# The end of a four-layer image kernel: result transposes cut into pieces, scaled products ahead of the shift, and three result parts stored as one transfer each

## The chip, the cores and the metric

The kernel runs on one core of one Trainium2 chip. The metric is the device time of one execution in microseconds (us), of which the median over several executions is taken. For the kernel before there are three: 2442.64, 2442.99 and 2450.58 us, so the median is 2442.99 us.

## The reference

Four layers work on an image batch `x` of shape (4, 64, 64, 64), float32: a self-attention over the 4096 tokens of each image, a gated convolution block, a second attention, and a non-local block. Only the end of the last layer is touched here:

```python
y = jnp.einsum('bnm,bmd->bnd', f, g_x).reshape(B, H, W, INNER)   # f: softmax of theta . phi
w_y = jnp.einsum('bhwd,dc->bhwc', y, w_W) + w_b
mean = jnp.mean(w_y, axis=(0, 1, 2))
var = jnp.var(w_y, axis=(0, 1, 2))
w_y = gamma * (w_y - mean) * jax.lax.rsqrt(var + EPS) + beta
return x + w_y
```

The mean and the variance run over all four images. So nothing can be stored before the last projection (`w_y`) of the last image is there; after that, all 4.19 MB of the result have to be scaled, shifted, added to `x`, turned and written to HBM.

## The kernel before

**Tiles.** `X` holds the input of the last layer for all four images, channels on partitions: 128 partitions (two halves `p` of the image by 64 channels) by 2048 columns for each image. `wys[b]` holds `w_y` in the same way. The result is cut into eight parts, two for each image: part `i` is 1024 columns of image `i // 2`. The result lies in HBM with the channel last, so each part must be turned by TensorE in eight blocks of 128x128 before it is stored.

**PSUM.** One tile `PS` of 128x4096 is dealt out in slots of 1024 columns. `take_slots` says which slots the next `new_ps` calls go round; the fourth slot serves `new_acc` for small sums.

**The end, in order.** `close_last` (line 1773) finishes the last 512 columns of the last image in two halves of 256: the softmax divisor by Ln and Exp on ScalarE (L1779, L1780), three VectorE operations (L1784 to L1787), the projection on TensorE (`project`, L1756), the bias on ScalarE (L1790), and the statistics on VectorE (L1796). `finish` (line 1898) joins the statistics (L1901), sends them through TensorE to get both halves' values (L1903, L1904), and makes `scale` and `shift`, one number for each channel (L1910 to L1920).

**The first three parts** go a different way from the other five. Their blocks of `X` are turned early: `begin_out` (line 1882) multiplies each block by the identity into a PSUM slot and leaves the sum open (`stop=False`). It is called for part 0 in `close_last` before the projections (L1781), for part 1 at the start of `finish` (L1899), for part 2 after the small products (L1908). When `scale` is there, `end_out` (line 1929) adds each block of `w_y` times `dscale`, the diagonal matrix of `scale`, to the same sum (L1931); `dshift`, the diagonal matrix of `shift`, times `ones` gives the shift along a row (`acc2`, L1989), and `add_shift` (line 1953) adds it on VectorE (L1957) into an SBUF tile `o` and stores that.

**The other five parts** are scaled and shifted on ScalarE (L1986), added to `X` on VectorE (`add`, L1974), turned on TensorE (`turn_out`, L1981), copied to SBUF (L2004, and L2007 and L2009 for the last), and stored.

**Stores.** `store` (line 1936) builds the destination `dst` with the dimensions p (2), h (64), q (8), n (128). In HBM a step of p is 2048 elements, a step of h is 4096, and q and n together are 1024 neighbouring elements, 4 KB. In the tiles of the first three parts the 128 partitions are p outside and h inside; in the tiles of the other five, `by_p` puts h outside and p inside. For the first three, two transfers of 64 partitions each are issued from SP's queue (L1940):

```python
for p in range(2):
    nc.sync.dma_start(
        out=dst[p].rearrange("h q n -> h (q n)"), in_=o[64 * p : 64 * p + 64, 0:1024]
    )
```

For the others it is one transfer of 128 partitions with h outside and p inside (L1944), from SP's queue for parts 3 and 5 and ScalarE's for 4 and 6, and two halves for part 7 (L1948), one from each queue.

**Order.** Every engine runs its instructions in the order in which the code issues them (a manual schedule for TensorE, ScalarE, VectorE and GpSimd). After `finish` each engine loads the flag `bad` (L2023) and branches around a fallback path (L2024), then the core's engines meet at the end (L2059).

Of the kernel before, what the change touches and what calls it, by code (L numbers as in the profile page):

```python
# [691 lines left out]
def fast_path(ctx: ExitStack, tc: tile.TileContext, a: dict, out: bass.AP, bad):  # L692
    nc = tc.nc
# [50 lines left out]
    def new_acc():  # L744
        turn_of["acc"] += 1
        return PS[:, bass.ts(6 + turn_of["acc"] % 2, 512)]
# [92 lines left out]
    for nm in names64 + names32:  # L839
        n = flat[nm].shape[0]  # L840
# [788 lines left out]
    def layer3(b):  # L1629
# [123 lines left out]
        def project(yz, ps, c0, cols):  # L1753
            for k in range(4):
                s, jj = k // 2, k % 2
                mm(  # L1756
                    ps[64 * s : 64 * s + 64, 512 * jj : 512 * jj + c0], wo[32 * k : 32 * k + 32, :],
                    yz[32 * k : 32 * k + 32, cols], start=True, stop=True,
                )
# [13 lines left out]
        def close_last():  # L1773
            yz, inv, wy = new_t("yz"), new_t("inv"), wys[b][:, 1024:2048].rearrange("p (j n) -> p j n", j=2)
            inside(0, sums0.rearrange("p b t -> p (b t)"), LO, HI)
            inside(1, sums2.rearrange("p b t -> p (b t)"), LO, HI)
            for i in range(2):
                r = inv[:, bass.ts(i, 256)]
                act(r, st["z"][:, bass.ts(i, 256)], AF.Ln)  # L1779
                act(r, r, AF.Exp, scale=-1.0)  # L1780
            early.append(begin_out(0))  # L1781
            for i in range(2):
                cols, r, d = bass.ts(i, 256), inv[:, bass.ts(i, 256)], inv[:, 512 + 256 * i : 768 + 256 * i]
                nc.vector.tensor_mul(d, st["z"][:, cols], r)  # L1784
                k = 2 * b + 1 + i
                stt(d, d, -2.0, r, ALU.add, ALU.mult, accum_out=inv3[:, k : k + 1])
                stt(yz[:, cols], d, -1.0, st["y"][:, cols], ALU.mult, ALU.mult)  # L1787
                ps = new_ps()
                project(yz, ps, 256, cols)
                act(  # L1790
                    wy[:, :, cols], ps.rearrange("p (j n) -> p j n", j=2)[:, :, 0:256],
                    AF.Identity, bias=V("L3_conv_w_b"),
                )
            inside(2, inv3, -1.0 / LO, 0.0)
            for i in range(2):
                nc.vector.bn_stats(bst[:, b, 1, i, :], wy[:, :, bass.ts(i, 256)])  # L1796
# [82 lines left out]

    def begin_out(i):
        b, g = i // 2, i % 2
        if i == 0:
            take_slots(0, 1, 2)
        ps = new_ps()
        if i == 0:
            take_slots(1, 2)
        elif i == 2:
            take_slots(0, 1, 2)  # L1890
        for k in range(8):
            mm(
                ps[:, bass.ts(k, 128)], X[:, b, 1024 * g + 128 * k : 1024 * g + 128 * k + 128], ident,
                start=k % 4 == 0, stop=False,
            )
        return ps

    def finish():
        early.append(begin_out(1))  # L1899
        mv = sm.tile([128, 2], F32, tag="mv", name="mv")  # L1900
        nc.vector.bn_aggr(mv, bst.rearrange("p b n i s -> p (b n i s)"))  # L1901
        acc = new_acc()
        mm(acc[:, 0:2], half[:, 0:128], mv, start=True, stop=True)  # L1903
        mm(acc[:, 2:3], half[:, 128:256], mv[:, 0:1], start=True, stop=True)  # L1904
        inside(3, mv[:, 1:2], 0.0, HI)
        found = new_acc()
        mm(found[0:1, 0:4], ones[:, 0:1], good, start=True, stop=True)
        early.append(begin_out(2))  # L1908
        mean = sm.tile([128, 4], F32, tag="mean", name="mean")
        nc.vector.tensor_copy(mean[:, 0:3], acc[:, 0:3])  # L1910
        stt(mean[:, 3:4], mean[:, 2:3], mean[:, 2:3], mean[:, 1:2], ALU.mult, ALU.add)
        rstd = sm.tile([128, 1], F32, tag="rstd", name="rstd")
        act(rstd, mean[:, 3:4], AF.Ln, bias=eps3)
        act(rstd, rstd, AF.Exp, scale=-0.5)
        mg = sm.tile([128, 1], F32, tag="mg", name="mg")
        stt(mg, mean[:, 0:1], -1.0, V("L3_conv_gamma"), ALU.mult, ALU.mult)
        scale = sm.tile([128, 1], F32, tag="scale", name="scale")
        nc.vector.tensor_mul(scale, rstd, V("L3_conv_gamma"))
        shift = sm.tile([128, 1], F32, tag="shift", name="shift")
        stt(shift, rstd, mg, V("L3_conv_beta"), ALU.mult, ALU.add)  # L1920
        t = new_t("diag")
        dscale, dshift, shifts = t[:, 0:128], t[:, 128:256], t[:, 256:384]
        nc.vector.tensor_scalar_mul(dshift, ident, shift)
        nc.vector.tensor_scalar_mul(dscale, ident, scale)

        def part(i):
            return X[:, i // 2, bass.ts(i % 2, 1024)], wys[i // 2][:, bass.ts(i % 2, 1024)]

        def end_out(i):
            for k in range(8):  # L1930
                mm(  # L1931
                    early[i][:, bass.ts(k, 128)], part(i)[1][:, bass.ts(k, 128)], dscale,
                    start=False, stop=k % 4 == 3,
                )

        def store(i, o, half_=None):
            dst = out[i // 2].rearrange(by_rows, p=2, q=16)[:, :, bass.ts(i % 2, 8)]
            if i < E:
                for p in range(2):
                    nc.sync.dma_start(  # L1940
                        out=dst[p].rearrange("h q n -> h (q n)"), in_=o[64 * p : 64 * p + 64, 0:1024]
                    )
            elif half_ is None:
                (nc.sync if i % 2 else nc.scalar).dma_start(  # L1944
                    out=dst.rearrange("p h q n -> h p (q n)"), in_=o[:, 0:1024]
                )
            else:
                (nc.scalar if half_ else nc.sync).dma_start(  # L1948
                    out=dst[:, :, bass.ts(half_, 4)].rearrange("p h q n -> h p (q n)"),
                    in_=o[:, bass.ts(half_, 512)],  # L1950
                )

        def add_shift(i):
            o = new_e("o")
            if i == 0:
                nc.vector.tensor_copy(shifts, acc2[:, 0:128])
            nc.vector.tensor_add(  # L1957
                o[:, 0:1024].rearrange("p (k n) -> p k n", n=128),
                early[i].rearrange("p (k n) -> p k n", n=128),
                shifts.unsqueeze(1).to_broadcast([128, 8, 128]),  # L1960
            )
            store(i, o)

        def by_p(x):
            return x.rearrange("c (q p h) -> c q p h", p=2, h=H)

        E, os, pss = len(early), {}, {}

        def add(i):
            if i == 2 * B - 2:  # L1970
                os["last"] = new_big("o")
            os[i] = new_e("o") if i < 2 * B - 2 else os["last"][:, bass.ts(i % 2, 2048)]
            xs, ws = part(i)
            nc.vector.tensor_add(  # L1974
                os[i][:, 1024:2048].rearrange("c (q h p) -> c q p h", p=2, h=H), by_p(xs), by_p(ws)
            )

        def turn_out(i):
            pss[i] = new_ps()
            for k in range(8):  # L1980
                nc.tensor.transpose(  # L1981
                    pss[i][:, bass.ts(k, 128)], os[i][:, 1024 + 128 * k : 1152 + 128 * k], ident
                )

        for i in range(E, 2 * B):
            act(part(i)[1], part(i)[1], AF.Identity, bias=shift, scale=scale)  # L1986
        acc2 = new_acc()
        for o in range(2):
            mm(acc2[64 * o : 64 * o + 64, 0:128], ones, dshift, start=True, stop=True)  # L1989
        end_out(0)  # L1990
        end_out(1)
        end_out(2)
        for i in range(E):
            add(E + i)
            add_shift(i)
            if i == 0:
                nc.vector.tensor_reduce(cnt, found[0:1, 0:4], AX.X, ALU.add)
                nc.vector.tensor_scalar(bad, cnt, -1.0, float(counted[0]), ALU.mult, ALU.add)
        for i in range(E, 2 * B):
            turn_out(i)  # L2000
            if i + E < 2 * B:
                add(i + E)
            if i < 2 * B - 1:
                nc.scalar.copy(os[i][:, 0:1024], pss[i])  # L2004
                store(i, os[i])
        i = 2 * B - 1
        nc.vector.tensor_copy(os[i][:, 0:512], pss[i][:, 0:512])  # L2007
        store(i, os[i], 0)
        nc.scalar.copy(os[i][:, 512:1024], pss[i][:, 512:1024])  # L2009
        store(i, os[i], 1)  # L2010
# [52 lines left out]
```

## Time and profile before

| What | us |
|---|---|
| median of three runs | 2442.99 |
| the profiled execution's own time | 2444.88 |
| its span in the trace | 2443.1 |
| last exponentials done (ACT L1657), end | 2408.5 |
| first TensorE block of part 0 (L1892), start | 2412.64 |
| last statistics joined (DVE L1901), start | 2417.39 |
| `shift` ready and ScalarE's scaling begins (ACT L1986) | 2420.01 |
| last compute (ACT L2009), end | 2433.50 |

Times in the table from the third row on are counted from the span's start. TensorE is busy for 2410.9 us of the span (99%), but the stretch that the change touches is the last 30 us, in which the engines wait for each other and, after 2433.5 us, only transfers, branches and the final meeting are left. How to read it: find which instruction each stage waits for last, and then ask of the transfers when they start, how many of the 16 DMA engines carry them, and at what rate.

### The profile page before, as it was taken

How to read it: one execution, taken by the hardware profiler on the slowest of the kernel's cores; microseconds unless marked ns; L12 is line 12 of the kernel's file. 1: busy time of each engine (PE TensorE's matmuls, PEld its weight loads, DVE VectorE, ACT ScalarE, POOL GpSimd, SP SyncE). 2: the span in 40 equal slices, each digit the busy share in tenths (PEclk: the TensorE clock that was granted, in tenths of full speed). 3: DMA queues.
4: the chain of work that ended last, by engine and by line, in shares of the span. 5: the costliest groups of instructions: out<-in, count | busy, mean ns of one | idle time of the engine just before them, and what ended most of it. 6: DMA issues, size and time to landing. Idle time of an engine off the chain costs nothing.

```text
span 2443.1 us, 63650 instructions
## 1 busy us (share of the span) xinstructions
PE 2410.9 (99%) x27509; PEld 914.5 (37%) x27509; DVE 1477.5 (60%) x1794; ACT 1642.9 (67%) x3140; POOL 541.1 (22%) x381
## 2 busy tenths in 40 slices
PE   9999999999999999999999999999999999999998
PEld 3343453336333543343344442144421344421113
DVE  2020278227732774278657668876668866688886
ACT  4656766666666666668655459954479744569996
POOL 2000000000000000030136561256631365622110
PEclk9999999999999999999999999999999999999999
DMA  3000000000000000030540027610075300386554
GB/s 80 1 18 1 19 1 18 18 19 1 19 18 5 15 19 18 21 76 2 118 92 19 20 64 138 139 28 23 16 152 118 79 22 21 76 169 141 118 116 117
DMA packets 66373, 131.68 MB, mean 54 GB/s; under 512 B 12860, under 2 KB 34085, under 8 KB 66085
## 3 DMA queue, kind: packets, MB, share of 16 engines
q0 software_dynamic: 23024, 81.83, 16.6%
q1 hardware_dynamic: 42309, 43.85, 7.9%
q8 instruction: 218, 3.57, 0.6%
q10 hardware_dynamic: 752, 1.85, 0.2%
q14 instruction: 70, 0.57, 0.1%
HBM read 4.80 MB, written 4.19 MB: 4 GB/s over the span
## 4 chain that ended last, share of the span: by engine, by line
PE 87%; DVE 5%; ACT 4%; DMA 1%; issue 1%; SPq 1%; POOL 0%; ACTq 0%; DVEq 0%; POOLq 0%
PE PS L1096 18%; PE PS L1122 18%; PE PS L1391 10%; PE PS L1453 10%; PE PS L1646 8%; PE PS L1707 8%; PE PS L1479 7%; PE PS L1206 2%; DVE tg L1698 2%; ACT e L1657 2%; DMA xn<-e 1%; ACT e L1396 1%; PE PS L1064 1%; PE PS L1171 1%; PE PS L1270 1%
## 5 line engine op out<-in xcount | busy, mean ns | idle before, releaser
L1101 ACT ACTIVATE e<-PS 128x1024 f32<-128x1024 f32 x512 | 523.7, 1023 | 339.8 <-PE PS L1096 306.5
L1396 ACT ACTIVATE e<-PS 128x512 f32<-128x512 f32 x632 | 370.9, 595 | 330.2 <-PE PS L1391 312.5
L1096 PE MATMUL PS<-X,q 64*64 64x512 f32 x4096 | 574.0, 591 | 2.3 <-DVE X L979 1.7
L1122 PE MATMUL PS<-e,vq 64*64 64x512 f32 x4096 | 575.3, 592 | 0.0
L1657 ACT ACTIVATE e<-PS 128x512 f32<-128x512 f32 (+2 forms) x588 | 500.1, 920 | 60.3 <-PE PS L1646 38.0
L1698 DVE TENSOR_TENSOR tg<-tg,e 128x2048 f32<-128x2048 f32 x172 | 393.9, 2290 | 42.7 <-ACT e L1657 31.3
L1391 PE MATMUL PS<-ko 64*64 64x512 f32 x2528 | 335.6, 596 | 1.7 <-ACT ko L1313 0.8
L1453 PE MATMUL PS<-e,X 64*64 64x512 f32 x2528 | 329.6, 590 | 1.1 <-ACT own L1465 1.1
L1432 POOL TENSOR_TENSOR esum<-esum,e 128x1024 f32<-128x1024 f32 x132 | 314.1, 2380 | 60.0 <-ACT e L1396 52.7
L1241 DVE SCALAR_TENSOR_TENSOR y<-pad,vec,y 128x1024 f32<-128x1024 f32 x240 | 308.9, 1287 | 18.2 <-ACT y L1237 10.9
L1432 POOL TENSOR_TENSOR esum<-e 128x1024 f32<-128x1024 f32 x22 | 52.2, 2373 | 1192.5 <-ACT e L1396 1184.7
L1409 DVE STREAM_TRANSPOSE turned<-e 128x1024 f32<-128x1024 f32 x196 | 240.6, 1238 | 107.5 <-ACT e L1396 107.2
L1646 PE MATMUL PS<-tg,ph 32*64 32x512 f32 x4096 | 295.7, 612 | 2.5 <-ACT e L1657 1.6
L1096 PEld LDWEIGHTS PS<-X,q 64*64 64x64 f32 x4096 | 183.0, 133 | 261.6 <-issue 181.5
L1122 PEld LDWEIGHTS PS<-e,vq 64*64 64x64 f32 x4096 | 183.1, 133 | 253.7 <-issue 158.5
L1707 PE MATMUL PS<-e,tg 128*32 128x512 f32 x2048 | 272.5, 604 | 0.0
L1109 DVE TENSOR_REDUCE sums<-zs 128x1 f32<-128x4 f32 x128 | 19.7, 154 | 276.0 <-ACT e L1101 275.9
L1679 POOL DMA_DIRECT2D xn<-e x116 | 101.0, 892 | 293.9 <-ACT e L1657 203.1
L1453 PEld LDWEIGHTS PS<-e,X 64*64 64x64 f32 x2528 | 98.0, 133 | 174.7 <-issue 155.1
L1391 PEld LDWEIGHTS PS<-ko 64*64 64x64 f32 x2528 | 90.3, 132 | 169.1 <-issue 145.1
L1646 PEld LDWEIGHTS PS<-tg,ph 32*64 32x64 f32 x4096 | 63.3, 129 | 224.4 <-ACT e L1657 192.0
L1396 ACT ACTIVATION_READ_ACCUMULATOR e<-PS 128x1 f32 x632 | 127.1, 201 | 0.0
(219 smaller groups left out, 1682.2 us busy)
## 6 DMA issues: line engine op xcount, KB each, us to landing
xn<-e POOLq DMA_DIRECT2D x132, 512.0 KB, 5.2
esum<-e POOLq DMA_DIRECT2D x20, 512.0 KB, 5.8
xn<-t SPq DMA_DIRECT2D x64, 128.0 KB
ph<-tg SPq DMA_DIRECT2D x64, 128.0 KB
xn<-X SPq DMA_DIRECT2D x224, 32.0 KB
xr<-X SPq DMA_DIRECT2D x176, 32.0 KB
ko<-ko SPq DMA_DIRECT2D x32, 128.0 KB
xr<-in_x_dram SPq DMA_DIRECT2D x13, 256.0 KB
```

The source lines that it names most:

```text
L1096: mm(ps[64 * c : 64 * c + 64, bass.ts(r, 512)], m.q[rows_, 128 * t + 64 * c : 128 * t + 64 * c + 64], x[rows_, bass.ts(g, 512)], start=Tru ...
L1101: act(es[g // 2][:, bass.ts(g % 2, 1024)], ps, AF.Exp, bias=SHIFT0, accum_out=zs[:, g : g + 1],)
L1122: ins = mm(PS[64 * s : 64 * s + 64, 2048 + 512 * j : 2560 + 512 * j], vq[rows_, :], es[j // 2][rows_, k : k + 512], start=t == 0 and i < 2 ...
L1241: stt(y1, win, wt, y1, ALU.mult, ALU.add)
L1391: mm(ps[64 * c : 64 * c + 64, bass.ts(r, 512)], m.ko[rows_, k : k + 64], m.ko[rows_, bass.ts(h, 512)], start=True, stop=True,)
L1396: act(e[:, bass.ts(r, 512)], ps[:, bass.ts(r, 512)], AF.Exp, bias=SHIFT2, accum_out=slot(g, 2 * u + r),)
L1432: nc.gpsimd.tensor_add(esum, st["e"][mine_t[h][0]] if k == 1 else esum, e)
L1453: mm(st["acc"][r][64 * c : 64 * c + 64, :], xw[rows_, 4 * g + 2 * u + c, :], st["e"][n][rows_, bass.ts(c, 512)], start=n == mine[h][0], st ...
L1646: mm(PS[64 * c : 64 * c + 64, bass.ts(banks[k], 512)], m.ph[32 * k : 32 * k + 32, 128 * mc + 64 * c : 128 * mc + 64 * c + 64], m.th[32 * k ...
L1657: act(e[:, 512 * lo : 512 * k], PS[:, 512 * banks[lo] : 512 * banks[lo] + 512 * (k - lo)], AF.Exp,)
L1698: nc.vector.tensor_add(esum, esum, e)
L1707: mm(st["y"][32 * k : 32 * k + 32, :], m.gx[:, i % 32, :], es[i][:, bass.ts(k, 512)], start=mc == 0, stop=i % 32 == 31,)
```

## The change

It has three edits.

First, part 0's eight blocks are no longer turned in one go before the last projections. Three are turned there, two after the first projection's products, three after the second's. A new function `go_on_out` issues blocks `lo` to `hi`; `begin_out` takes the number of blocks to begin with.

Second, in `finish`: part 2 begins with six blocks instead of eight; `dscale` is made before `dshift`; the first four scaled products of part 0 are issued before the shift's sum `acc2`, and the other four after it; part 2's last two blocks follow, and then part 1's and part 2's scaled products as before.

Third, in `store`: for the first three parts the two transfers of 64 partitions become one transfer of 128, still from SP's queue, with the destination's dimensions in the order p, h.

```diff
-            early.append(begin_out(0))
+            early.append(begin_out(0, 3))
...
                 project(yz, ps, 256, cols)
+                go_on_out(0, early[0], 3 + 2 * i, 5 + 3 * i)
...
-    def begin_out(i):
+    def begin_out(i, upto=8):
...
-        for k in range(8):
+        go_on_out(i, ps, 0, upto)
+        return ps
+
+    def go_on_out(i, ps, lo, hi):
+        b, g = i // 2, i % 2
+        for k in range(lo, hi):
             mm(
-                ps[:, bass.ts(k, 128)], X[:, b, 1024 * g + 128 * k : 1024 * g + 128 * k + 128], ident,
+                ps[:, bass.ts(k, 128)],
+                X[:, b, 1024 * g + 128 * k : 1024 * g + 128 * k + 128], ident,
                 start=k % 4 == 0, stop=False,
             )
-        return ps
...
-        early.append(begin_out(2))
+        early.append(begin_out(2, 6))
...
+        nc.vector.tensor_scalar_mul(dscale, ident, scale)
         nc.vector.tensor_scalar_mul(dshift, ident, shift)
-        nc.vector.tensor_scalar_mul(dscale, ident, scale)
...
-        def end_out(i):
-            for k in range(8):
+        def end_out(i, lo=0, hi=8):
+            for k in range(lo, hi):
...
             if i < E:
-                for p in range(2):
-                    nc.sync.dma_start(
-                        out=dst[p].rearrange("h q n -> h (q n)"), in_=o[64 * p : 64 * p + 64, 0:1024]
-                    )
+                nc.sync.dma_start(out=dst.rearrange("p h q n -> p h (q n)"), in_=o[:, 0:1024])
...
         acc2 = new_acc()
+        end_out(0, 0, 4)
         for o in range(2):
             mm(acc2[64 * o : 64 * o + 64, 0:128], ones, dshift, start=True, stop=True)
-        end_out(0)
+        end_out(0, 4, 8)
+        go_on_out(2, early[2], 6, 8)
         end_out(1)
         end_out(2)
```

## The prediction, made before the changed kernel was run

> **What bounds the kernel now.** I read the page first, then the order of time over the last 30 us, then the DMA share by stretches. The page says what has to leave:
>
> ```profile
> HBM read 4.80 MB, written 4.19 MB: 4 GB/s over the span
> ```
>
> All 4.19 MB are the result (8 parts of 524,288 B), and all of it goes out after the statistics. The order of time shows the stages before that:
>
> ```profile
> 2412.64 2.05 PE L1892 MATMUL PS<-ident,X 128*128 128x128 f32 x16
> ...
> 2414.45 0.42 DVE L1787 SCALAR_TENSOR_TENSOR yz<-inv,PS 128x256 f32<-128x256 f32 x1
> ...
> 2414.62 1.09 PE L1756 MATMUL PS<-yz,wo 32*64 32x256 f32 x16
> ...
> 2416.09 2.05 PE L1892 MATMUL PS<-ident,X 128*128 128x128 f32 x16 [0.38 <-ACT wy L1790]
> 2417.39 0.59 DVE L1901 BATCH_NORM_AGGREGATE mv<-bst 128x2 f32<-128x96 f32 x1
> ...
> 2418.03 0.38 PE L1903 MATMUL PS<-mv,half 128*128 128x2 f32 x2
> ...
> 2420.67 0.44 PE L1989 MATMUL PS<-diag,ones 128*64 128x128 f32 x4
> ...
> 2423.13 1.22 DVE L1957 TENSOR_TENSOR o<-PS,diag 128x1024 f32<-128x1024 f32 x1 [0.41 <-PE PS L1931]
> ...
> 2424.38 5.87 SPq L1940 DMA_DIRECT2D out_dram<-o  x6
> ...
> 2433.54 0.95 ACTq L1948 DMA_DIRECT2D out_dram<-o  x1
> ```
>
> See that L1903 starts at 2418.03, where the statistics (2417.39 + 0.59 = 2417.98) and TensorE's second set of blocks end together: both limit it. And the last store is issued at 2433.5, almost 10 us before the end. What fills those 10 us is in the stretches (columns: length, the engines' busy time, granted clock, share of the 16 DMA engines, GB/s):
>
> ```profile
> 2424.00:2425.50 1.50, 1.50 (x16) 1.50 (x15) 1.47 (x4) 1.50 (x2) 0.00 (x0) 1.00 0.00 0
> 2425.50:2432.00 6.50, 5.54 (x48) 4.88 (x46) 5.89 (x6) 3.73 (x5) 0.00 (x0) 1.00 0.90 216
> 2434.50:2439.00 4.50, 0.00 (x0) 0.00 (x0) 0.00 (x0) 0.00 (x0) 0.00 (x0) 0.71 1.01 397
> 2439.50:2443.10 3.60, 0.00 (x0) 0.00 (x0) 0.00 (x0) 0.00 (x0) 0.00 (x0) 0.50 0.05 19
> ```
>
> The DMA engines are full from 2425.5 to about 2439.5: the end is bound by draining the stores. They drain at 216 GB/s while the 64-partition stores (L1940) run, and at 397 GB/s on 128-partition ones, 397 / (16 x 1.01) = 24.6 GB/s for each engine. From the first issue (2424.38) to the first bytes (2425.5) is 1.1 us; from the last bulk bytes (2439.5) to the end 3.6 us, with ScalarE's first instruction after its branch at 2440.9 and SP's last wait there at 2441.4.
>
> [...] the outermost sizes are 64 or, with h outside and p inside at equal steps of 2048 elements, 128, and the share of 0.90 to 1.01 shows them on all 16.
>
> **The change, part by part.**
>
> *First edit (blocks in pieces).* One block is 2.0 / 8 = 0.25 us of TensorE. Three end at 2412.64 + 0.74 = 2413.38. The first `yz` is ready at 2413.61 (L1787 began at 2413.19), so the first projection runs at 2413.66 instead of 2414.62, about 0.40 us to issue and 0.70 to its end; two blocks follow to 2414.56. The second `yz` is ready at 2414.87 (2414.45 + 0.42), the second projection issues until 2415.32, three blocks run to 2416.06, part 1's eight to 2418.04. The bias and the second statistics end 0.4 us earlier (projection's end 2415.62, plus 0.68 for L1790, 0.65 for L1796, then 0.59 for L1901: 2417.6), but L1903 stands behind the blocks on TensorE: 2418.06, against 2418.03. Worth nothing; what is late in place of the statistics is TensorE.
>
> *Second edit (order around the shift).* Part 2's six blocks end at 2418.7 + 1.49 = 2420.2; `dscale`, now first, is ready at 2420.01 + 0.29 = 2420.30. Four scaled products, 8 instructions of 0.113 us (48 in 5.43), run from 2420.34 to 2421.24, `acc2` takes 0.37, the other four end at 2422.5, plus 0.2 until VectorE sees them: 2422.7 instead of 2423.13. VectorE is free for it (its L1974 ends at 2422.43 and the copy of the shifts costs 0.28, to 2422.7). The first store is issued at 2424.0 instead of 2424.38. The two blocks moved behind (0.5 us) make part 1's products end at 2425.0, before VectorE wants them (2425.3), and TensorE is done with them at 2426.6, as before (2426.50). Gain 0.4 us on the stores' start.
>
> *Third edit (one transfer).* Three of SP's six issues of 0.47 to 0.60 us go; that queue is not what the stores wait for. What counts is the pattern: source 128 partitions, destination 2 (p), 64 (h), 1024. With p outside the two cannot join into one dimension (p steps 2048, h 4096). [...] two engines. They are the same two for all three transfers, and each of them also carries its sixteenth of every other part. Load of one of the two: 3 x 262,144 + 5 x 32,768 = 950,272 B. At 24.6 GB/s that is 38.6 us. First bytes at 2424.0 + 1.1 = 2425.1, last at 2463.7. [...] After the last bytes SP's wait and the engines' meeting cost about 2.4 us: the last bytes ahead of SP's last wait move between 2440.5 and 2441.0 (20 GB/s in that half microsecond), 2.1 to 2.6 us before the end at 2443.1. Sum: span 2466.1 against 2443.1, **+23.0 us**. The branches (ScalarE's is over at 2440.9 now) are done long before that.
>
> The rate is not shown for two engines alone. [...] From below: [...] 216 / (16 x 0.90) = 15.0 GB/s, 63.4 us, 2490.9. I take 24.6[...].
>
> The profiled execution took 2444.88 us, its span 2443.1, the median is 2442.99; I add the 23.0 to the median: 2466.0.
>
> **The rivals.**
>
> *All sixteen engines carry the joined transfers (not slower).* If the pattern is dealt out by its 128 rows of 4 KB, the three parts leave at 397 GB/s, 1.3 us each, and VectorE makes one every 2.3 us: the backlog is gone. Parts 2, 3 and 4 then pile up from 2429.9, and six parts (3.15 MB, 7.9 us) end at 2437.8 instead of 2439.5, a gain of 1.7 us if ScalarE's branch does not hold the end; with its last store issued 0.4 us earlier, it holds it to that: 2441.3 to 2442.6, I take 2442.0. It decides from the point where the destination counts as 128. For it: the halved rate of L1940. Against: [...] the care with which the other five parts get h outside. It is no change that could be measured.
>
> *Two engines, but a queue that stands still.* [...] SP and ScalarE may be held in their issues until the first transfers have drained. For it: SP's L1944 takes 1.3 to 1.7 us against 0.34 to 0.36 on ScalarE, a queue already pushed back. The sum on the two engines stays; held issues add one start of 1.1 us for each of the late stores, at most 4: up to 2470. [...]
>
> *Clearly faster.* The last store is issued at 2433.1 at the earliest, plus 1.1 to its first bytes, 0.7 us for its 262,144 B and 2.4: 2437.3, 5.7 us less. Below the bound in the next part, so even that would not count as faster.
>
> **How the numbers follow.** A measurement of this kernel can tell about 0.3%, 7.3 us, from no change. Two engines at about the full rate of one: 0.75. Two engines with held issues or a lower rate: 0.10. Sixteen engines: 0.14, within the bound. Faster beyond it: 0.01. So slower 0.85, same 0.14, faster 0.01. The range is 2458 [...] to 2486 (a little inside the lowest rate); the first two cases hold most of their 0.85 in it.
>
> **What would show it.** Right: three L1940-like issues with the first at 2424.0; a DMA share of about 0.12 to 0.13 (2 of 16) and near 50 GB/s from some 2440 to 2463; L1903 unmoved near 2418.0; L1957 0.4 us earlier. Wrong: a share near 1 with some 390 GB/s right from 2425, and an end near 2442.

## The result, and the profile after

The changed kernel takes 2465.92 us (median of 6 runs, 2465.39 to 2468.17) against 2442.81 us for the kernel before in the same series: 23.1 us more, ratio 1.0087, 95% interval 1.0077 to 1.0097. The profiled execution has a span of 2464.0 us.

First the stretches of the changed kernel's end, with the columns of the stretches in the prediction (the last two are the share of the 16 DMA engines and GB/s):

```profile
2422.00:2423.00 1.00, 1.00 (x12) 1.00 (x11) 1.00 (x2) 1.00 (x2) 0.00 (x0) 1.00 0.00 0
...
2425.00:2426.00 1.00, 1.00 (x12) 1.00 (x10) 1.00 (x2) 0.51 (x1) 0.00 (x0) 1.00 0.13 33
...
2431.00:2432.00 1.00, 0.00 (x0) 0.00 (x0) 0.00 (x0) 0.00 (x0) 0.00 (x0) 1.00 0.95 369
...
2444.00:2445.00 1.00, 0.00 (x0) 0.00 (x0) 0.00 (x0) 0.00 (x0) 0.00 (x0) 0.50 0.13 53
...
2447.00:2448.00 1.00, 0.00 (x0) 0.00 (x0) 0.00 (x0) 0.00 (x0) 0.00 (x0) 0.50 1.01 397
...
2455.00:2456.00 1.00, 0.00 (x0) 0.00 (x0) 0.00 (x0) 0.00 (x0) 0.00 (x0) 0.50 0.13 53
...
2461.00:2462.00 1.00, 0.00 (x0) 0.00 (x0) 0.00 (x0) 0.00 (x0) 0.00 (x0) 0.50 0.04 14
```

A share of 0.13 is 2 of 16. The other parts leave in bursts (between 2428 and 2440, and again around 2447). Outside the bursts two engines work alone: 33 GB/s together at first (2425), 53 GB/s later (2444, 2455). In the kernel before, the share stood at 0.90 to 1.01 on average until almost everything was out.

Then the order of time of the changed kernel (start, length; PEld is TensorE's weight load, SPq and ACTq are issues of transfers by SP and ScalarE, x2 is two of them with the time between):

```profile
2415.74 0.30 PEld L1909 LDWEIGHTS PS<-mv,half 128*128 128x128 f32 x2
2415.85 0.28 PE L1909 MATMUL PS<-mv,half 128*128 128x2 f32 x2
...
2420.60 1.23 DVE L1960 TENSOR_TENSOR o<-PS,diag 128x1024 f32<-128x1024 f32 x1 [0.17 <-PE PS L1937]
...
2421.85 3.12 SPq L1945 DMA_DIRECT2D out_dram<-o  x2
...
2426.53 7.68 SPq L1947 DMA_DIRECT2D out_dram<-o  x1
...
2434.31 1.19 SPq L1945 DMA_DIRECT2D out_dram<-o  x1
2435.60 10.86 SPq L1947 DMA_DIRECT2D out_dram<-o  x1
2437.49 0.34 ACTq L1951 DMA_DIRECT2D out_dram<-o  x1
2446.55 1.27 SPq L1951 DMA_DIRECT2D out_dram<-o  x1
```

L1945 is the joined store, L1947 that of a later part. SP sits in one issue for 7.68 and in another for 10.86 us. SP's order is not written by hand as that of the other engines is: part 3's store (the first L1947) went ahead of part 2's (the second L1945 line).

This profile's end begins earlier than that of the kernel before: the first logarithm (L1779) starts at 2408.83, there at 2411.06. That difference arose ahead of everything the change touches; over the profiled executions below, whose programs are the same up to there, that start lies between 2408.83 and 2415.74. So I compare the ends from that instruction on (the anchor). All numbers are us after L1779's start, each a difference of two times of one trace:

| Kernel | statistics through TensorE (weight load starts) | first store issued | last copy ends | end of span |
|---|---|---|---|---|
| before | 6.97 | 13.32 | 22.44 | 32.04 |
| changed | 6.91 | 13.02 | 22.17 | 55.17 |
| first two edits alone | 6.91 | 13.02 | 22.16 | 32.26 |
| third edit alone | 6.98 | 13.33 | 22.46 | 55.53 |
| one part joined | 6.91 | 13.02 | 22.18 | 37.15 |
| late stores on ScalarE | 6.91 | 13.02 | 24.01 | 55.10 |
| halves from SP and GpSimd | 6.90 | 13.02 | 22.16 | 32.67 |
| halves from SP and ScalarE | 6.91 | 13.01 | 23.62 | 31.62 |
| joined, from GpSimd | 6.91 | 13.29 | 22.15 | 48.59 |
| joined, h outside | 6.91 | 13.02 | 22.16 | 30.62 |

From the anchor the change costs 55.17 - 32.04 = 23.13 us, as the medians say. Each row is a single execution: the ends of the kernels whose medians cannot be told from the kernel before's (the rows before, first two edits alone, and halves from two queues) lie between 31.62 and 32.67, so a difference of less than about 1 us in that column says little.

### The profile page after: what moved, and what is told of

The parts are those of the page before. It is cut to its first block, busy times and chain, and to the rows that moved or that the text cites. A ratio compares the mean times of both kernels' runs of the same rounds, so it can differ in the third digit from the quotient of the medians.

```text
span 2464.0 us, 63647 instructions
## 1 busy us (share of the span) xinstructions
PE 2409.5 (98%) x27509; PEld 914.6 (37%) x27509; DVE 1477.4 (60%) x1794; ACT 1644.2 (67%) x3140; POOL 541.9 (22%) x381
## 3 DMA queue, kind: packets, MB, share of 16 engines
q0 software_dynamic: 23024, 81.83, 16.5%
## 4 chain that ended last, share of the span: by engine, by line
PE 88%; DVE 5%; ACT 4%; issue 1%; SPq 0%; DMA 0%; DVEq 0%; ACTq 0%
PE PS L1096 18%; PE PS L1122 18%; PE PS L1391 10%; PE PS L1453 10%; PE PS L1646 9%; PE PS L1707 8%; PE PS L1479 7%; DVE tg L1698 2%; PE PS L1206 2%; ACT e L1657 2%; ACT e L1396 1%; PE PS L1171 1%; PE PS L1270 1%; PE PS L1561 1%; PE PS L1064 1%
```

## The experiments

Each run is the changed kernel with the edit shown, unless it says otherwise.

**The first two edits alone**

```diff
-                nc.sync.dma_start(out=dst.rearrange("p h q n -> p h (q n)"), in_=o[:, 0:1024])
+                for p in range(2):
+                    nc.sync.dma_start(
+                        out=dst[p].rearrange("h q n -> h (q n)"), in_=o[64 * p : 64 * p + 64, 0:1024]
+                    )
```

> First and second edit kept, the stores as before (two transfers of 64 partitions for each of the first three parts). Theory (two DMA engines carry each joined transfer, and that is the whole loss): the end comes back, 2442.4 us, within 1 us of the kernel before; the first store issued about 0.4 us earlier in relation to the last exponential, L1909 (the statistics through TensorE) unmoved in relation to it. Rival (the order on TensorE costs something too): 2445 us or more.

Measured: 2444.63 us, ratio 1.0004 (0.9998 to 1.0011) to the 2444.03 us of the kernel before in this series. The loss is gone. The first store goes out 0.30 us earlier (13.02 against 13.32); no gain shows at the end (32.26 against 32.04). So the 23 us belong to the third edit, and the order on TensorE costs nothing that can be measured.

**The third edit alone**, in the kernel before: the diff above the other way round.

> The kernel before with the third edit alone. Theory: 0.4 us above the changed kernel, 2466.3 us, ratio 1.0095, and a DMA share of 0.12 to 0.14 with 50 to 55 GB/s at the end. Rival (the first two edits bear part of the loss): clearly under 2466, such as 2455.

Measured: 2467.36 us, ratio 1.0103 (1.0087 to 1.0118). The whole loss is there without the other two edits. The end lies 0.36 us later than in the changed kernel (55.53 against 55.17), where the first store goes out 0.31 us earlier. That fits a drain that starts with the first store and sets the end, but a single trace of each does not show it.

**One part joined**

```diff
-            if i < E:
+            if i < 1:
                 nc.sync.dma_start(out=dst.rearrange("p h q n -> p h (q n)"), in_=o[:, 0:1024])
+            elif i < E:
+                for p in range(2):
...
```

> The changed kernel, with only part 0 stored as one transfer, parts 1 and 2 as two of 64 partitions each. Theory (the load of the two engines): they carry 262,144 + 7 x 32,768 = 491,520 B; at the 24.8 GB/s of each that the changed kernel showed (950,272 B from 2423.0 to 2461.3) that is 19.8 us instead of 38.3, so 18.5 us less than the changed kernel: 2447.4, 4.6 us above the kernel before. Rival (a fixed price, once, for the pattern or for a queue that stands still): the loss stays above 15 us. Rival (a third of the loss for each part): 7.7 us above, 2450.5.

Measured: 2448.58 us, ratio 1.0019 (1.0010 to 1.0028), 4.6 us more than the kernel before. From the anchor the end comes 18.0 us earlier than with three joined (37.15 against 55.17); the load of the two engines said 18.5. A price paid once would have left most of the loss; a third for each part would have given 7.7 us, outside the interval (2.4 to 6.8 us). One joined part costs little because most of its 262,144 B on each of the two engines (some 10 us at 26.5 GB/s, an estimate) leave while the other parts drain. This run alone does not separate the load from issues that are held: two issues of SP take 8.92 us together here, and a last burst at 375 to 381 GB/s runs until 2443.5, two microseconds before the last bytes (2445.6). The next run separates them.

**Late stores on ScalarE**

```diff
-                (nc.sync if i % 2 else nc.scalar).dma_start(
+                nc.scalar.dma_start(
...
-                (nc.scalar if half_ else nc.sync).dma_start(
+                nc.scalar.dma_start(
```

> The changed kernel, with the stores of parts 3, 5 and the first half of 7 issued from ScalarE's queue, so that nothing stands behind the joined transfers on SP's queue. Theory (the two engines' bytes): the same bytes, the same end, 2465.5 to 2467 us, and these parts' bytes gone by about 2438. Rival (held issues on SP set the end): several us less than the changed kernel, 2460 or under.

Measured: 2467.59 us, ratio 1.0101 (1.0086 to 1.0116); from the anchor 55.10 against 55.17. The stretches of this kernel:

```profile
2429.00:2430.00 1.00, 0.93 (x8) 0.86 (x8) 0.20 (x1) 0.55 (x1) 0.00 (x0) 1.00 1.00 401
...
2436.00:2437.00 1.00, 0.00 (x0) 0.00 (x0) 0.00 (x0) 0.00 (x0) 0.00 (x0) 0.50 0.13 53
...
2450.00:2451.00 1.00, 0.00 (x0) 0.00 (x0) 0.00 (x0) 0.00 (x0) 0.00 (x0) 0.50 0.13 53
...
2461.00:2462.00 1.00, 0.00 (x0) 0.00 (x0) 0.00 (x0) 0.00 (x0) 0.00 (x0) 0.50 0.09 37
```

Nothing of a later part stands behind the joined stores on SP any more; nearly all parts leave from 2427 to 2436 (193 to 401 GB/s until 2435), only the last half part follows in a burst at 2440, and the two engines still work until 2462. ScalarE's last store still goes out late here (issued at 2439.40, its copy ended at 2432.91), but it is the burst at 2440, long before the end. The held issues are real, but they are not what sets the end. The bytes on two engines are.

**Joined, from GpSimd's queue**

```diff
-                nc.sync.dma_start(out=dst.rearrange("p h q n -> p h (q n)"), in_=o[:, 0:1024])
+                nc.gpsimd.dma_start(out=dst.rearrange("p h q n -> p h (q n)"), in_=o[:, 0:1024])
```

> The changed kernel with the three joined transfers issued from GpSimd's queue instead of SP's. Theory[...]: each transfer is still on two engines, but on another pair, so the loads lie beside each other: the last pair ends about (262,144 + some 100,000 B) / 24.8 GB/s = 14.6 us after part 2's first bytes, 3 to 7 us above the kernel before, with a DMA share of 0.25 to 0.4 between. Rival (always the same two engines): 2466 us as the changed kernel. Rival (GpSimd deals the 128 rows to all engines): at or below the kernel before.

Measured: 2459.91 us, ratio 1.0067 (1.0051 to 1.0082), 16.4 us more than the kernel before; I expected 3 to 7. The DMA rows from 2422 to 2462 (all packets; queue: packets, MB, share of 16 engines; issue: KB each, median us to landing) and two stretches of this kernel:

```profile
DMA packets 3992, 4.29 MB, mean 107 GB/s; under 512 B 2832, under 2 KB 2832, under 8 KB 3984
...
q0 software_dynamic: 3120, 1.58, 15.4%
...
out_dram<-o POOLq DMA_DIRECT2D x3, 512.0 KB, 23.3
```

```profile
2426.00:2427.00 1.00, 1.00 (x12) 1.00 (x11) 1.00 (x2) 0.03 (x1) 0.83 (x1) 1.00 0.17 45
...
2442.00:2443.00 1.00, 0.00 (x0) 0.00 (x0) 0.00 (x0) 0.00 (x0) 0.00 (x0) 0.50 0.36 135
```

The share of 0.36 is near six of 16 (0.375), where the changed kernel shows 0.13: it fits three transfers on three pairs, beside each other, instead of piled on one. That part of the expectation held. Two other parts did not.

The drain is longer. Counted so, each of the six engines carries 262,144 B and its sixteenths of the other five parts, 163,840 B, not the "some 100,000" of the expectation: 425,984 B, 17.2 us at 24.8 GB/s instead of 14.6. From part 2's first bytes (issued at 2428.36, so near 2429.8) to the last bytes (just before 2451) it took about 21 us, an estimate of 20 GB/s for each engine; why it is not 24.8 is not shown. The rows are not cut. A mean of 1.58 MB / 3120 = 506 B a packet misleads: from 2 KB to 8 KB the view has 3984 - 2832 = 1152 packets, 768 of them rows of the other five parts and 384 the three parts' rows of 4 KB, whole. The rest of the 3120 are small packets beside them, and what those cost is not shown either.

And the end comes 8 us after the last bytes, against 2.4 us in the changed kernel. GpSimd stands in one wait of 22.1 us that ends at 2451.8, just behind the last bytes; then its closing steps take 1.3 us (INC_SWDGE_SEM, L2029) and 4.8 us (DRAIN, L2064), to 2458.1, before the engines' meeting can end. In the changed kernel, where GpSimd issues no late store, it is through with the same two by 2429.5, while the transfers still run. Of the 16.6 us from the anchor (48.59 against 32.04), some 6 are this close and the rest is the longer drain.

**Halves from two queues at once**, p = 1 from GpSimd's queue or from ScalarE's:

```diff
-                nc.sync.dma_start(out=dst.rearrange("p h q n -> p h (q n)"), in_=o[:, 0:1024])
+                for p in range(2):
+                    (nc.gpsimd if p else nc.sync).dma_start(
+                        out=dst[p].rearrange("h q n -> h (q n)"), in_=o[64 * p : 64 * p + 64, 0:1024]
+                    )
```

> First and second edit kept; each of the first three parts stored as two transfers of 64 partitions, p = 0 from SP's queue and p = 1 from GpSimd's, so that both halves are under way at once. Theory [...]: the first parts leave at 300 GB/s or more instead of 216, the bulk is gone by about 1 to 2 us earlier, and the end is 0.5 to 1.7 us before the variant with the first two edits alone: 2441 to 2442.5 where that is 2442.6. Rival (two transfers of halves serialize from whatever queue): 216 GB/s as before and no change within 0.5 us.

> As the variant with SP and GpSimd, but p = 1 from ScalarE's queue. Theory: the same rate on the DMA engines, but part 2's issue stands ahead of ScalarE's copies of parts 3 and 4 (L2009) and waits for VectorE, so these copies start 1 to 1.5 us later and the gain is given back: within 1 us of the kernel before. Rival (ScalarE's issues cost nothing): like the variant with GpSimd.

Measured: with GpSimd 2444.86 us, ratio 0.9999 (0.9991 to 1.0008); with ScalarE 2443.93 us, ratio 1.0000 (0.9992 to 1.0009). With ScalarE both halves of part 0 are issued within 0.01 us (2425.59 on SP, 2425.60 on ScalarE), and the stretches of that kernel show:

```profile
2426.98:2428.58 1.60, 1.60 (x17) 1.60 (x16) 1.60 (x2) 0.27 (x1) 0.00 (x0) 1.00 0.93 215
2428.58:2430.58 2.00, 1.68 (x16) 1.45 (x15) 2.00 (x3) 0.00 (x0) 0.00 (x0) 1.00 0.83 201
```

The engines are busy for 0.93 and 0.83 of the time and the rate is still that of one half at a time (216 GB/s in the prediction's lines). Counted by queue (q10 is ScalarE's, q1 SP's; packets, MB, share), from 2426.5 to 2428.1 only the 64 rows of ScalarE's half leave, although SP's half was issued as well:

```profile
q10 hardware_dynamic: 64, 0.26, 84.6%
```

From 2428.1 to 2429.2 it is SP's half, and of ScalarE's queue only small packets:

```profile
q1 hardware_dynamic: 80, 0.26, 64.8%
...
q10 hardware_dynamic: 16, 0.00, 0.8%
```

My theory for these two runs was wrong: two 64-partition transfers under way at once did not add up. With ScalarE their bytes left one after the other; with GpSimd the rate from 2427.03 to 2428.63 was 220 GB/s at a share of 0.94, not the 300 or more that I expected. Why a transfer of 64 partitions moves at about half the rate of one of 128 is not shown. ScalarE's last copy does end 1.5 us later than with GpSimd (23.62 against 22.16), as expected, yet no loss shows at the end (31.62).

**Joined, with h outside**

```diff
-                nc.sync.dma_start(out=dst.rearrange("p h q n -> p h (q n)"), in_=o[:, 0:1024])
+                nc.sync.dma_start(out=dst.rearrange("p h q n -> h p (q n)"), in_=o[:, 0:1024])
```

> The changed kernel, with the joined transfer's destination walked with h outside and p inside, as the other five parts do: one dimension of 128 steps of 2048 elements. The rows of the first three parts land with p and h exchanged (the result's order of rows in these parts is left out); bytes, transfers and issues are the changed kernel's. Theory (only the destination's outermost size of 2 costs, not joining as such): a DMA share of 0.9 or more with 300 to 400 GB/s on the first parts, and the whole loss gone; the end 0.4 to 1.7 us before the kernel before, 2441.1 to 2442.4 where that is 2442.8, ratio 0.9993 to 0.9998. Rival (joining 128 partitions from SP's queue is slow in itself): 2455 us or more. Rival (the drain's end is set by other work anyway): ratio 0.9999 to 1.0005.

Measured: 2442.01 us, ratio 0.9992 (0.9984 to 1.0000) to 2444.45 us; from the anchor the end at 30.62, 1.4 us before that of the kernel before and 24.6 us before that of the changed kernel. Its stretches:

```profile
2423.98:2424.98 1.00, 1.00 (x11) 1.00 (x10) 1.00 (x2) 0.67 (x1) 0.00 (x0) 1.00 0.99 401
2424.98:2425.98 1.00, 1.00 (x11) 1.00 (x10) 1.00 (x2) 0.00 (x0) 0.00 (x0) 1.00 0.21 78
2425.98:2426.98 1.00, 1.00 (x11) 1.00 (x10) 1.00 (x2) 0.34 (x1) 0.00 (x0) 1.00 0.66 266
```

Same bytes, same queue, same issue, same 128 partitions; only the order of two dimensions of the destination differs. Part 0 is gone in some 1.3 us at 401 GB/s, and the engines wait for part 1. So joining as such was not slow here (401 GB/s, a share of 0.99); with 2 outermost it was (33 to 53 GB/s, 0.13).

The packets that the profiles count on SP's queue (packets, MB, share) say the same in another way. In the kernel before, in this one and in the changed kernel they are:

```profile
q1 hardware_dynamic: 42309, 43.85, 7.9%
q1 hardware_dynamic: 42261, 43.85, 7.9%
q1 hardware_dynamic: 42219, 43.85, 7.8%
```

The bytes are equal. Three transfers fewer make 48 packets fewer here, 16 for each transfer that is gone. The changed kernel has as many transfers as this one and 42 packets fewer again, 14 for each joined transfer: 2 are left of the 16. Packets under 512 B over the three ends are 192, 144 and 102: 12 x 16, 9 x 16, and 6 x 16 + 3 x 2. That fits one small packet for each engine that carries a part of a transfer.

This run also shows about what the third edit could have been worth on all engines: 1.4 us from the anchor and 2.4 us by the medians, with an interval of 0 to 3.9 us, so at the edge of the noise, where the edit as made costs 23. It is no version to keep, since its rows lie wrong; a tile of the first parts with h outside, which would make it right, was not tried. No other version beat the kernel before.

## Why the prediction was right

**Two engines by the destination's outermost size**: right, but an assumption of mine: no store of the kernel before has an outermost size below 64, so none of them shows two engines, nor that they would be the same two for all three parts. The share of 0.13, the packet counts, the run with h outside and the unchanged end with the late stores on ScalarE settle it. The runs have outermost sizes of 2, 64 and 128 only; what other sizes do is not shown.

**Load and rate**: the load was right, the rate right on average. The sum on one engine, 950,272 B, took from 2423.1 to about 2461.6, 38.5 us or 24.7 GB/s, where I took 24.6 and 38.6. But the average hides two rates: 33 GB/s for both in the first microseconds (2425), 53 later (2444, 2455), 16.5 and 26.5 each. So the rate of one engine among sixteen, which I took over for two alone, did not hold at the start, and later the two ran faster than it. At 26.5 throughout, the sum would have taken 35.9 us. That the two deviations cancel to a tenth of a microsecond is luck; why the engines start slowly is not shown.

**First bytes 1.1 us after the issue, 2.4 us after the last bytes**: the issue was at 2421.85, the first bytes fall into the stretch after 2423.0; from the last bytes, shortly after 2461.5, to the end at 2464.0 it is 2.4. Right.

**First edit worth nothing**: right. The statistics join earlier (L1907 begins 6.05 us after the anchor against 6.33), but the products through TensorE move by 0.06 only (6.91 against 6.97): TensorE's blocks are last there. No run has this edit alone; the order of time shows it.

**Second edit 0.4 us on the first store**: 0.30. The scaled products took 0.1 us longer to reach VectorE than I had summed. Whether it reaches the end no run can tell: in the first two edits alone no gain shows, and the third edit with and without them differs by 0.36 us in one trace each.

**Held issues**: they were held, up to 10.86 us, and cost nothing that shows at the end (55.17 with the late stores behind them, 55.10 without), as the prediction's sum on the two engines implied. The rival that gave them up to 4 us more has fallen.

**All sixteen engines**, had it been so: I gave 2442.0 us; the run with h outside measured 2442.01, in a series in which the kernel before stood 1.6 us higher, so the equal figures are chance: the gain was 1.4 to 2.4 us, at the edge of the noise, and I had put it at 1.0.

**Clearly faster**: its sum gives 5.8 us, not 5.7; nothing hangs on that.

## What to carry to other kernels

Before joining stores, write down both access patterns as the transfer walks them and look at the slowest dimension: here 128 partitions on one side did not help where the other began with 2. The stores with 64 outermost showed a DMA share of 0.93 (first two edits alone, 2430.14 to 2431.74), those with 128 outermost 0.99 (h outside), those with 2 outermost 0.13, two of 16 engines. And where the end of a kernel is a drain, price an edit by the load of the busiest DMA engine, not by the number of issues saved.

## What the runs showed of the hardware that was not expected

SP was held inside a single issue for 7.68 and 10.86 us while transfers on two engines were under way; in the kernel before, its issues of the same two parts took 1.71 and 1.27 us. ScalarE's issues took 0.34 to 0.36 us each, but its last one began only at 2437.49, 6.5 us after its copy had ended (2431.00), where in the kernel before it follows at once (2433.54 after 2433.50); what it waited for is not shown.

Two engines alone moved 16.5 GB/s each in the first microseconds and 26.5 GB/s each later.

Three stores with 2 outermost from GpSimd's queue showed a share of 0.36, which fits three pairs of engines, and the kernel ended 8 us after the last bytes, as GpSimd's own closing steps of 1.3 and 4.8 us came behind its last transfer.

Two stores of 64 partitions, issued within 0.01 us from two queues, went one after the other, at 201 to 215 GB/s, while one of 128 partitions moved 401.
